# A four-layer graph network on one core: the norm's last step tied behind masks, three kinds of transposes later, half of the feature sums later

## The chip, the cores and the metric

The kernel runs on one core of one Trainium2 chip. The time is the device time of one execution in microseconds (us); a comparison uses the median of several executions. The kernel before has a median of 2874.45 us over three runs (2873.52 to 2877.68).

Five engines work in parallel, each through its own queue in a fixed order: TensorE (PE, matmuls; PEld is its weight load), VectorE (DVE), ScalarE (ACT), GpSimd (POOL) and SyncE (SP, which here only issues transfers). An instruction that has to wait for another engine or for a transfer also holds everything behind it in its own queue. In what follows, times such as "at 2463.23" are microseconds from the start of the profiled execution, and L354 is line 354 of the kernel before.

## The reference

There are 2708 nodes with 512 features each, and a dense 2708 x 2708 matrix `adj`, mostly zeros. Four layers follow each other, each of the form `x = layernorm(x + layer(x))`. Cut to what matters:

```
deg = max(sum(adj != 0, axis=1), 1)
# layer 0: weighted sum over neighbours; each non-zero gets 1/sqrt(count) added
head = mask(adj > 0) / sqrt(row count);  inc = adj + head
y0 = (inc @ x) / rowsum(inc)
# layer 1: attention over the non-zeros, a second convolution, two gates
h = x @ W_sa;  s_left = h @ a[:512];  s_right = h @ a[512:]
e = where(adj != 0, exp(-leaky_relu(s_left[:,None] + s_right[None,:])), 0)
y1 = sigmoid(gate_a * (e @ h / (rowsum(e) + 1e-5)) + gate_b * (adj @ (x @ W_gcn) + b_gcn))
# layer 2: three hops
p = x;  out = x @ w[0];  for i in 1..3: p = adj @ p; out += p @ w[i]
# layer 3: normalised convolution with self loops
y3 = relu((D^-1/2 (adj + I) D^-1/2 @ x + x) @ W + b)
```

Everything is in 32-bit floats. The products of `adj` (or of something of its shape) with a 2708 x 512 matrix are by far the largest part.

## The kernel before, in words

**Products.** The nodes are split in two halves of 1354, the features in two halves of 256. So `adj` is a 2 x 2 array of blocks (called 11, 12, 21, 22 in the code), and the features are four blocks B11, B12, B21, B22. A product of two such arrays is done in the manner of Strassen and Winograd, with seven block products in place of eight. For that, sums of blocks are needed on both sides: of the features (T1 to T4, made on VectorE), and of the adjacency (called z, s or a, made from loaded tiles on VectorE, L403 and L1226). T1 = B12 - B11, T2 = B22 - T1, T3 = B22 - B12 (it takes the place of B12), T4 = B21 - T2. In the tiles, a name such as T3A is the part A of the rows of T3.

**Stages.** A stage is a sweep over ranges of columns of the result; `S[s]` is 28 s on an axis of positions. Layer 0 is the sweep at S[0] (about 0 to 430 us), layer 1 has two sweeps at S[1] and S[2] (430 to 1300 us), the hops and layer 3 are sweeps of a second kind (`sweep2`, at S[3] to S[6]), which splits the rows once more with a second level of seven products; the last, S[6], is from about 2490 us to the end. Its range of 338 columns is processed as group g, product j, with `u` the length of one step.

**Order.** Each piece of work is an event, put down with `at(pos, fn, hold)`. Events are sorted by position and emitted in that order. For the first part of the list (positions below START = 5, and what follows up to three times as many instructions) each engine's queue is in the order of the list. Behind it, the scheduler sets the order, with the list as priority; an event with `hold=True` is tied behind the instruction before it in the list on the same engine. The order is fixed when the kernel is built, and every execution replays it.

**The pieces that the change touches:**

- `next_x2(base, ...)` loads the next sweep's features, and `sums(g)` (L346 to L357) makes T1, T2, T3, T4 of one part g = A, C, B, D in one event, by four subtractions L352 to L355 on VectorE, held at position base + 4.2 + 0.3 i.
- `sweep(...)`, with `plain` for the first range of layer 0: `pw` is the position of the preparing instructions of its blocks "21" and "22" (L779 and L780: a weight row times a tile, and its sum with the tile, on VectorE).
- `layernorm(dsts, y, w, on_scalar)` (L553 to L567): statistics on VectorE (L555, L557, L559), a power on POOL (L560), a product on VectorE (L562), and the last step either on ScalarE (L565) or on VectorE (L567). `done0` calls it for each finished tile of layer 0, after adding the product (L838), and stores the tile in X1.
- Counting in layer 0: masks of the non-zeros are made on ScalarE (L712, L713) or VectorE (L710); TensorE sums them (cnt, L724); the result becomes a row of roots, r (L753), which `spread_row` transposes on TensorE (pr, L761) and copies on ScalarE (row, L764) for L779 of the next range.
- In layer 1, `score_rows` and `rows` (in `extra1`) both call `to_rows`: a transpose on TensorE (ps_r, L937) of the scores s_left (L929) or of the reciprocal degrees rdeg (L999), a copy on ScalarE (L939) and a store from POOL (L940).
- In `sweep2`, L1217 loads z, `add_diag` (L1240) adds the diagonal to it, L1226 makes the sums z and s, L1260 those of the features (t), L1281 are the matmuls into the accumulators accu, accc, accd, acca, and L1299 and L1305 take these out into q. L1317 adds two q. The rest of the rows goes through accr (L1352, L1356) and is added in L1363. ps_n (L1388) is a transpose of a finished q for the norm; L635, L645 and L654 are the dense products of the last layer (d or q, ps, z).

Of the kernel before, what the change touches and what calls it, by code (L numbers as in the profile page):

```python
# [24 lines left out]
ALU = mybir.AluOpType  # L25
# [43 lines left out]
def gnn_kernel(ctx: ExitStack, tc: tile.TileContext, x, adjT, w_sa, a_sa, w_gcn, b_gcn, wab, bab, w_hop, w_out,  # L69
# [232 lines left out]
    def next_x2(base, src, ext_src=None, one=False, plus=False, swapped=False):  # L302

        q = nc.gpsimd
        m = RANGES2[1][0] // P
        early = {"B11": (-5.8, m), "B12": (-4.8, m)}
        late = 2.3 if base == S[6] else 1.6
        if one:
            early["B22"] = (-0.95, RANGES[-1][0] // P)

        def go(s, ks, ext):
            for k in ks:
                x_load(src, k, s, q)
            if ext and ext_src is not None:
                c0 = HD if s in ("B12", "B22") else 0
                for i, g in enumerate("BD"):
                    r0 = (HD if s in ("B21", "B22") else 0) + i * P
                    h = "T3" if s == "B12" else s
                    if g == "D" and ks[-1] < 8:
                        group(h, g)  # L320
                    t, w = groups[h, g][0][:, 2, :], ext_src[r0 : r0 + P, :]
                    if not swapped:
                        nc.scalar.dma_start(out=t, in_=w[:, c0 : c0 + HD])
                        continue
                    for f in range(2):
                        nc.scalar.dma_start(out=t[:, f * P : (f + 1) * P].rearrange("p (c d) -> p c d", d=32),
                                            in_=w.rearrange("p (c f d) -> p f c d", c=4, d=32)[:, c0 // P + f, :, :])

        def residual(s):

            for i, g in enumerate("BD"):
                t = groups[s, g][0][:, 2, i * P : (i + 1) * P]
                nc.vector.tensor_tensor(t, t, ident, ALU.add)

        if plus:
            at(base - 1.4, lambda: residual("B22"), True)
            at(base + 1.9, lambda: residual("B11"), True)
        for s, p in (("B22", 0.0 if one else -1.95), ("B21", 0.02), ("B11", late), ("B12", late + 0.15)):
            ks = list(range(KW))
            if s in early:  # L340
                lo, m = early[s]
                at(base + lo, lambda s=s, m=m: go(s, range(m), True))
                ks = range(m, KW)
            at(base + p, lambda s=s, ks=ks: go(s, ks, ks[0] == 0))

        def sums(g):  # L346
            i = slice(0, 2 if g in "BD" and ext_src is None else 3)
            part = lambda t: t[:, i, :]
            for s in ("T1", "T2", "T4"):
                group(s, g)  # L350
            t = {s: part(groups[s, g][0]) for s in SETS}
            nc.vector.tensor_tensor(t["T1"], t["T3"], t["B11"], ALU.subtract)  # L352
            nc.vector.tensor_tensor(t["T2"], t["B22"], t["T1"], ALU.subtract)
            nc.vector.tensor_tensor(t["T3"], t["B22"], t["T3"], ALU.subtract)  # L354
            nc.vector.tensor_tensor(t["T4"], t["B21"], t["T2"], ALU.subtract)  # L355
            for s in ("T1", "T2", "T3", "T4"):
                groups[s, g][1].update(range(3))  # L357

        def rest():
            for e in range(2):  # L360
                cols = slice(e * HD, (e + 1) * HD)
                for s in REST_HOMES[e]:
                    group(s, "R")
                t, t32 = (groups[s, "R"][0] for s in REST_HOMES[e])
                lo, hi = src[KT - 1], src[2 * KT - 1]
                rows_over(q, t, (lo[:, cols], hi[:, cols]))
                q.dma_start(out=t32, in_=copies(hi[KA - KR :, cols], 4))

        at(base + late + 0.15, rest)
        for i, g in enumerate("ACBD"):  # L370
            at(base + 4.2 + 0.3 * i, lambda g=g: sums(g), True)


    def sweep(base, ranges, prep=None, extra=None, done=None, first=False, late=None, sums=False, save=False):
        A, spare = {}, {}
        nk = KW
        for r, (R0, n) in enumerate(ranges):
# [34 lines left out]
            pw = {ij: (p + 0.3, f) for ij, (p, f) in when.items()}  # L412
            if plain:
                when = {"11": (-4.0, 0.2), "12": (-3.8, 0.2), "21": (-2.4, 0.4), "22": (-1.6, 0.4)}
                pw = {"11": (-0.9, 0.6), "12": (-0.3, 0.6), "21": (3.3, 0.9), "22": (4.1, 0.9)}
            for ij in ("11", "21", "22", "12"):
                for k in ks:
                    p, f = when[ij]
# [131 lines left out]
                     [(h * KT + k, k * P - R0, wt(k)) for k in ts])  # L550


    def layernorm(dsts, y, w, on_scalar=False):  # L553
        st = small.tile([P, 6], F32, name="st")
        nc.vector.bn_stats(st[:w], y[:w])  # L555
        mv = small.tile([P, 2], F32, name="mv")
# [5 lines left out]
            nc.vector.scalar_tensor_tensor(rstd[:w, 0:1], mv[:w, 0:1], -1.0, rstd[:w, 1:2], ALU.mult, ALU.mult)  # L562
        for d, c0, c1 in dsts:
            if on_scalar:
                nc.scalar.activation(d[:w], y[:w, c0:c1], AF.Identity, bias=rstd[:w, 0:1], scale=rstd[:w, 1:2])  # L565
                continue
            nc.vector.tensor_scalar(d[:w], y[:w, c0:c1], mv[:w, 0:1], rstd[:w, 1:2], ALU.subtract, ALU.mult)  # L567

# [226 lines left out]
    def extra0(pb, r, R0, n, A):  # L795
        if r == 0:
            for h, p, d in ((0, -3.7, 0.05), (1, 1.9, 0.055)):
# [9 lines left out]
                    at(pb + (1.7 if h == 0 else 4.8) + 0.06 * j,  # L807
                       lambda h=h, i=i, a=a: add_run(R0, h, n, count_rows(R0, i), a()))
                at(pb + p + d * 22, lambda h=h: count_row(R0, n, h))
                at(pb + p + d * 22 + 0.1 * h, lambda h=h: spread_row(R0, n, h))  # L810
        if r + 1 < len(RANGES0):
            R1, n1 = RANGES0[r + 1]
            for h, p, d in ((0, 1.0, 2.5), (1, 3.8, 2.5)) if r else ((0, 3.2, 2.2), (1, 5.4, 2.1)):
                for i in range(NT):
                    q = pb + p + d * i / NT
                    at(q - 0.7, lambda i=i, h=h: count_load(R1, n1, h, i))
                    at(q - 0.35, lambda i=i, h=h: count_mask(R1, n1, h, i))
                    count_three(q, R1, n1, h, range(NT), i)
                at(pb + p + d, lambda h=h: count_row(R1, n1, h))
                at(pb + p + d + 0.15, lambda h=h: spread_row(R1, n1, h))  # L820

        def inverse(o, s, t, w):
            nc.vector.reciprocal(o, s)
# [4 lines left out]
    def done0(p0, dp, last, R0, n, h, C, tiles):  # L828
        for i, (t, lo, w) in enumerate(tiles):
# [5 lines left out]
            def b(t=t, lo=lo, w=w, got=got):  # L835
                ps = untranspose(C, h, lo, w)
                y = got["x"]
                nc.vector.scalar_tensor_tensor(y[:w], ps[:w], rd[t][:w], y[:w], ALU.mult, ALU.add)  # L838
                o = targets(t, last and not h, "o")
                layernorm(o, y, w, not last)  # L840
                store(X1[t], o, w)

            p = p0 + dp * i + (0.0 if last and not h else 0.2)
            at(p - 0.3, a)
            at(p, b)

    def start0():
        ws = load_w(w_sa)
# [105 lines left out]
    i = 0  # L954
    for R0, n in RANGES:
        for h in (1, 0):
# [5 lines left out]
                at(S[1] + 1.1 + 0.95 * i, lambda t=h * KT + k, w=wt(k): score(t, w, got1))  # L962
                i += 1
            at(S[1] + 1.12 + 0.95 * (i - 1), lambda R0=R0, h=h, ts=tiles_of(R0, n): scores_end(R0, h, ts))
            at(S[1] + 1.6 + 0.95 * (i - 1), lambda R0=R0, h=h, ts=tiles_of(R0, n): score_rows(R0, h, ts))
    at(S[1] + 1.13 + 0.95 * (i - 1), scores_over)

    def extra1(pb, r, R0, n, A):
# [34 lines left out]
                    DROW[h][0, ts[0] * P : (ts[-1] + 1) * P].rearrange("(k i) -> k i", i=P))  # L1003

        at(pb + 2.6, lambda: end(1))
        at(pb + 3.2, lambda: rows(1))
        at(pb + 5.2, lambda: end(0))
        at(pb + 5.8, lambda: rows(0))

    def done1(p0, dp, last, R0, n, h, C, tiles):  # L1010
        Z = {}
# [183 lines left out]
    def sweep2(base, ext, done, on_diag=False):  # L1195
        nk = K2 + ext
        u = 2 / 7
        for g, (i0, n) in enumerate(RANGES2):
            Q, C = {}, {}
            for j, m in enumerate(ORDER2[g]):  # L1200
# [41 lines left out]

                for p, q, pos in ((0, 0, -0.52), (1, 0, -0.51), (1, 1, 0.59), (0, 1, 4.04)):
                    for k in range(nk) if on_diag and op != "12" else ():
                        at(b + u * (pos + 0.8 * k / nk), lambda p=p, q=q, k=k, f=add_diag: f(p, q, k))

                def tsum(nm, x, y, T=T, st=st, nk=nk):

# [366 lines left out]
```

## Time and profile before

| | us |
|---|---|
| median of 3 runs (lowest, highest) | 2874.45 (2873.52, 2877.68) |
| the profiled execution's own time | 2874.17 |
| its span, first to last instruction | 2872.1 |
| mean granted TensorE clock | 0.998 |
| TensorE busy | 2826.4 (98%) |
| VectorE busy | 2197.7 (77%) |
| ScalarE busy | 546.3 (19%) |
| POOL busy | 617.6 (22%) |
| longest single wait of TensorE | 4.4 |

Read the busy times first: they say which engine there is almost no room on. The list of waits then says for how long TensorE stood still, for which line of which engine, how often and how long at the longest. A line of a timeline gives the start, the duration, the engine, the line of the kernel, the operation, what it writes and reads, the shapes and how many like it follow each other; in brackets at its end is the idle time of the engine just before it and what ended that.

### The profile page before, as it was taken

Reading aid. Unit: us, or ns where it says so; the run is one execution under the profiler, and the core shown is the slowest. Engines: PE = TensorE matmul, PEld = TensorE weight load, DVE = VectorE, ACT = ScalarE, POOL = GpSimd, SP = SyncE. Lnnn points to the kernel's source line nnn. Section 1 sums busy time; section 2 is a strip of 40 time slices with the busy share of each in tenths; the row PEclk is TensorE's granted clock in tenths of the full one; section 3 lists DMA queues with packets and bytes.
Section 4 is the critical chain, followed back from the end, with each engine's and each line's share of the span. In section 5 each row is a group of like instructions: output and inputs, shape, how many; then the busy total and the mean of one; then the engine's idle time right before and its main releaser. Section 6 shows DMA issues by size and latency. Waiting matters only on the chain. (4 is left out here: it accounts for less than half of the span.)

```text
span 2872.1 us, 37476 instructions
## 1 busy us (share of the span) xinstructions
PE 2826.4 (98%) x10963; PEld 1870.2 (65%) x10963; DVE 2197.7 (77%) x5670; ACT 546.3 (19%) x1119; POOL 617.6 (22%) x1113
## 2 busy tenths in 40 slices
PE   7999999999999999999999999999999999999998
PEld 5656665658765656766666666666666666666665
DVE  6989799667636554655699788887888878799987
ACT  4554200101146444641100000000000100100001
POOL 0223233223310101123213033030330211501202
PEclk9999999999999999999999999999999999999999
DMA  7666466355534333565668667566675665754542
GB/s 232 204 200 191 143 213 225 114 163 167 191 107 135 111 115 97 168 193 153 202 203 242 204 193 239 172 209 197 198 234 173 187 196 177 228 172 146 177 141 92
DMA packets 368524, 510.04 MB, mean 178 GB/s; under 512 B 63424, under 2 KB 321700, under 8 KB 368320
## 3 DMA queue, kind: packets, MB, share of 16 engines
q1 hardware_dynamic: 302392, 370.56, 43.8%
q0 software_dynamic: 49344, 126.38, 13.1%
q10 hardware_dynamic: 16584, 10.71, 1.3%
q8 instruction: 87, 1.43, 0.2%
q14 instruction: 117, 0.96, 0.1%
HBM read 423.77 MB, written 83.65 MB: 177 GB/s over the span
## 5 line engine op out<-in xcount | busy, mean ns | idle before, releaser
L1226 DVE TENSOR_TENSOR z<-z 128x339 f32<-128x339 f32 (+1 forms) x966 | 454.6, 504 | 12.6 <-PE accu L1281 3.4
L1299 ACT COPY q<-accu 128x338 f32<-128x338 f32 (+1 forms) x84 | 34.6, 443 | 1004.5 <-PE accu L1281 1002.7
L560 POOL TENSOR_TENSOR rstd<-rstd,neg_half 128x1 f32<-128x1 f32 (+3 forms) x91 | 59.3, 652 | 755.8 <-DVE rstd L559 494.9
L1281 PE MATMUL accc<-s,t 128*128 128x338 f32 (+1 forms) x644 | 198.2, 450 | 0.0
L1281 PE MATMUL accu<-z,t 128*128 128x338 f32 (+1 forms) x644 | 194.0, 448 | 1.5 <-DVE z L1226 1.5
L1281 PE MATMUL accd<-z,t 128*128 128x338 f32 (+1 forms) x644 | 193.9, 448 | 0.6 <-DVE q L1363 0.6
L1281 PE MATMUL accc<-z,t 128*128 128x338 f32 (+1 forms) x644 | 193.5, 448 | 0.5 <-ACT q L1299 0.5
L1414 POOL DMA_DIRECT2D Y<-y x192 | 105.0, 553 | 366.7 <-DVE y L1409 333.7
L403 DVE TENSOR_TENSOR a<-a,a 128x384 f32<-128x384 f32 (+2 forms) x330 | 162.6, 511 | 22.5 <-PE accu L458 21.7
L1281 PEld LDWEIGHTS accc<-s,t 128*128 128x128 f32 x644 | 120.9, 190 | 64.1 <-issue 7.5
L1281 PEld LDWEIGHTS accc<-z,t 128*128 128x128 f32 x644 | 122.0, 190 | 61.6 <-issue 1.0
L1281 PEld LDWEIGHTS accu<-z,t 128*128 128x128 f32 x644 | 121.7, 190 | 61.7 <-DVE z L1226 2.0
L1281 PEld LDWEIGHTS accd<-z,t 128*128 128x128 f32 x644 | 121.9, 190 | 60.5 <-DVE q L1363 1.5
L1226 DVE TENSOR_TENSOR s<-z 128x338 f32<-128x338 f32 (+1 forms) x322 | 149.7, 503 | 12.7 <-PE accc L1281 8.4
L1305 DVE TENSOR_TENSOR q<-q,accd 128x338 f32<-128x338 f32 (+1 forms) x112 | 56.0, 500 | 115.1 <-PE accd L1281 115.1
L1082 DVE SCALAR_TENSOR_TENSOR a<-a,e 128x384 f32<-128x384 f32 (+2 forms) x160 | 77.4, 507 | 51.0 <-ACT e L1081 46.3
L1080 ACT ACTIVATE e<-row,s_right 128x384 f32<-128x384 f32 (+5 forms) x176 | 96.5, 569 | 76.1 <-PE accc L458 20.4
L979 DVE SCALAR_TENSOR_TENSOR deg<-a,deg 128x384 f32<-128x384 f32 (+2 forms) x152 | 75.8, 505 | 13.6 <-DMA a<-in_adjT 11.9
L406 POOL DMA_DIRECT2D As<-a x120 | 64.9, 544 | 73.0 <-DVE a L403 70.2
L779 DVE SCALAR_TENSOR_TENSOR s<-a,row 128x384 f32<-128x384 f32 (+2 forms) x152 | 75.1, 507 | 6.0 <-ACT row L764 6.0
L1081 ACT ACTIVATE e<-e 128x384 f32<-128x384 f32 (+5 forms) x176 | 79.4, 477 | 1.8
L606 PE MATMUL ps_d<-w,xT 128*128 128x512 f32 (+1 forms) x176 | 79.2, 593 | 0.4 <-ACT xT L597 0.4
(683 smaller groups left out, 5840.4 us busy)
## 6 DMA issues: line engine op xcount, KB each, us to landing
z<-As SPq DMA_DIRECT2D x320, 169.5 KB
z<-As SPq DMA_DIRECT2D x320, 169.0 KB
a<-in_adjT SPq DMA_DIRECT2D x240, 192.0 KB
z<-in_adjT SPq DMA_DIRECT2D x240, 169.5 KB
z<-in_adjT SPq DMA_DIRECT2D x240, 169.0 KB
a<-in_adjT SPq DMA_DIRECT2D x120, 165.0 KB
a<-in_adjT SPq DMA_DIRECT2D x112, 128.0 KB
As<-a POOLq DMA_DIRECT2D x60, 192.0 KB, 3.9
```

Of the source, the lines that this page charges most:

```text
L403: nc.vector.tensor_tensor(A[r, dst, k][:, :n], A[r, a, k][:, :n], A[r, b, k][:, :n], op)
L406: nc.gpsimd.dma_start(out=SD[m][k * P : (k + 1) * P, R0 : R0 + n], in_=A[r, dst, k][:, :n])
L560: nc.gpsimd.tensor_tensor(rstd[:w, 1:2], rstd[:w, 0:1], neg_half[:w], ALU.pow)
L606: nc.tensor.matmul(o, lhs(c), r, start=c == 0 and n == 0, stop=c == DC - 1, skip_group_check=True)
L779: nc.vector.scalar_tensor_tensor(t[:w, :n], a[:w, :n], 0.0, row[R0, h][:w, :n], ALU.is_gt, ALU.mult)
L979: nc.vector.scalar_tensor_tensor(d[:w, :n], a[:w, :n], 0.0, d[:w, :n], ALU.not_equal, ALU.add)
L1080: nc.scalar.activation(e[:w, :n], row[R0, h][:w, :n], AF.Prelu, bias=s_right[:w, t : t + 1], alpha=0.01)
L1081: nc.scalar.activation(e[:w, :n], e[:w, :n], AF.Exp, scale=-1.0)
L1082: nc.vector.scalar_tensor_tensor(a[:w, :n], a[:w, :n], 0.0, e[:w, :n], ALU.not_equal, ALU.mult)
L1226: nc.vector.tensor_tensor(d[:, :n], Z[x + (k,)][:, :n], Z[y + (k,)][:, :n], op)
L1281: nc.tensor.matmul(B[home][:, :n], stat(v, k), a[:, :n], start=bool(start and k == 0), stop=k == nk - 1, skip_group_check=True)
L1414: nc.gpsimd.dma_start(out=rows[:, :, f * P : (f + 1) * P], in_=o[32 * f : 32 * (f + 1), : m * P].rearrange("p (b d) -> p b d", d=P))
```

## The change

Six edits, all of them to positions and ties. No operation is added or removed.

1. `sums(g)` is split in three events: T1 and T2 stay at base + 4.2, T3 moves to base + 7.4, T4 to base + 9.2 (each + 0.3 i for the parts A, C, B, D), all held.
2. The preparing instructions of the blocks "21" and "22" of the first range are 0.1 later.
3. The last step of layer 0's norm (L565), where it is on ScalarE, becomes an event of its own at p + 0.28, held behind what stands before it on ScalarE; the store into X1 is put at the same position.
4. `spread_row` is later: by 0.08 for one of the two halves of the first range, by 0.1 and 0.25 for those of the next ranges.
5. In layer 1, `score_rows` goes from +1.6 to +2.3, and `rows` from +3.2 and +5.8 to +3.7 and +6.3.
6. In `sweep2`, `add_diag` of the very first product (g = j = 0) is held. Only S[6] has the diagonal on.

```diff
-        def sums(g):
+        def sums(g, n):
             i = slice(0, 2 if g in "BD" and ext_src is None else 3)
             part = lambda t: t[:, i, :]
-            for s in ("T1", "T2", "T4"):
-                group(s, g)
+            if n == 0:
+                for s in ("T1", "T2", "T4"):
+                    group(s, g)
             t = {s: part(groups[s, g][0]) for s in SETS}
-            nc.vector.tensor_tensor(t["T1"], t["T3"], t["B11"], ALU.subtract)
-            nc.vector.tensor_tensor(t["T2"], t["B22"], t["T1"], ALU.subtract)
-            nc.vector.tensor_tensor(t["T3"], t["B22"], t["T3"], ALU.subtract)
-            nc.vector.tensor_tensor(t["T4"], t["B21"], t["T2"], ALU.subtract)
-            for s in ("T1", "T2", "T3", "T4"):
-                groups[s, g][1].update(range(3))
+            if n == 0:
+                nc.vector.tensor_tensor(t["T1"], t["T3"], t["B11"], ALU.subtract)
+                nc.vector.tensor_tensor(t["T2"], t["B22"], t["T1"], ALU.subtract)
+                for s in ("T1", "T2", "T3", "T4"):
+                    groups[s, g][1].update(range(3))
+            elif n == 1:
+                nc.vector.tensor_tensor(t["T3"], t["B22"], t["T3"], ALU.subtract)
+            else:
+                nc.vector.tensor_tensor(t["T4"], t["B21"], t["T2"], ALU.subtract)
...
         for i, g in enumerate("ACBD"):
-            at(base + 4.2 + 0.3 * i, lambda g=g: sums(g), True)
+            for n, p in enumerate((4.2, 7.4, 9.2)):
+                at(base + p + 0.3 * i, lambda g=g, n=n: sums(g, n), True)
...
-                pw = {"11": (-0.9, 0.6), "12": (-0.3, 0.6), "21": (3.3, 0.9), "22": (4.1, 0.9)}
+                pw = {"11": (-0.9, 0.6), "12": (-0.3, 0.6), "21": (3.4, 0.9), "22": (4.2, 0.9)}
...
-    def layernorm(dsts, y, w, on_scalar=False):
+    def layernorm(dsts, y, w, on_scalar=False, late=None):
...
             if on_scalar:
-                nc.scalar.activation(d[:w], y[:w, c0:c1], AF.Identity, bias=rstd[:w, 0:1], scale=rstd[:w, 1:2])
+                fn = lambda d=d, c0=c0, c1=c1: nc.scalar.activation(d[:w], y[:w, c0:c1], AF.Identity,
+                                                                    bias=rstd[:w, 0:1], scale=rstd[:w, 1:2])
+                fn() if late is None else late.append(fn)
                 continue
...
-                at(pb + p + d * 22 + 0.1 * h, lambda h=h: spread_row(R0, n, h))
+                at(pb + p + d * 22 + 0.18 * h, lambda h=h: spread_row(R0, n, h))
...
-                at(pb + p + d + 0.15, lambda h=h: spread_row(R1, n1, h))
+                at(pb + p + d + (0.25 if h else 0.4), lambda h=h: spread_row(R1, n1, h))
...
-                o = targets(t, last and not h, "o")
-                layernorm(o, y, w, not last)
-                store(X1[t], o, w)
+                got["o"] = o = targets(t, last and not h, "o")
+                layernorm(o, y, w, not last, None if last else got.setdefault("late", []))
+                if last:
+                    store(X1[t], o, w)
+
+            def c(t=t, w=w, got=got):
+                for fn in got["late"]:
+                    fn()
...
+            if not last:
+                at(p + 0.28, c, True)
+                at(p + 0.28, lambda t=t, w=w, got=got: store(X1[t], got["o"], w))
...
-            at(S[1] + 1.6 + 0.95 * (i - 1), lambda R0=R0, h=h, ts=tiles_of(R0, n): score_rows(R0, h, ts))
+            at(S[1] + 2.3 + 0.95 * (i - 1), lambda R0=R0, h=h, ts=tiles_of(R0, n): score_rows(R0, h, ts))
...
-        at(pb + 3.2, lambda: rows(1))
+        at(pb + 3.7, lambda: rows(1))
...
-        at(pb + 5.8, lambda: rows(0))
+        at(pb + 6.3, lambda: rows(0))
...
-                        at(b + u * (pos + 0.8 * k / nk), lambda p=p, q=q, k=k, f=add_diag: f(p, q, k))
+                        at(b + u * (pos + 0.8 * k / nk), lambda p=p, q=q, k=k, f=add_diag: f(p, q, k), g == j == 0)
```

## The prediction

> **What bounds the kernel now.** I read the table of busy time first, then the list of what TensorE waited for, then the timelines of the places named there, and the granted clock by window.
>
> ```profile
> PE 2826.4 (98%) x10963; PEld 1870.2 (65%) x10963; DVE 2197.7 (77%) x5670; ACT 546.3 (19%) x1119; POOL 617.6 (22%) x1113
> ```
>
> TensorE is busy for 2826.4 of 2872.1 us, so an edit that only reorders work has 45.7 us to win at the very most. 7.4 us of these lie behind the last matmul. The changed kernel, built, has the same instructions, matched one to one, in another order within each engine's queue; what I say below of an order after the change is that built order. So everything hangs on the single waits:
>
> ```profile
> PE pr L761 <- DVE r L753: 5.7, 4, 2.0
> PE cnt L724 <- ACT mask L713: 3.6, 2, 2.6
> PE accd L1281 <- DVE z L1226: 2.5, 6, 1.0
> PE ps_n L1388 <- DVE q L1305: 1.8, 1, 1.8
> ...
> PE ps_r L937 <- DVE s_left L929: 1.6, 1, 1.6
> PE ps_r L937 <- DVE y L652: 1.6, 1, 1.6
> PE accu L1281 <- DVE z L1226: 1.5, 1, 1.5
> ...
> PE accd L1281 <- DVE q L1363: 0.6, 1, 0.6
> ```
>
> Columns: total us, times, longest. Each line is something that the diff moves or that stands beside it: 18.9 us in all. Why they arise shows on the other engines, with the idle time and its releaser in brackets (ScalarE, then VectorE):
>
> ```profile
> 75.47 0.81 ACT L565 ACTIVATE o<-ld,rstd 128x512 f32<-128x512 f32 x1 [2.90 <-DVE rstd L562]
> ...
> 81.31 0.81 ACT L565 ACTIVATE o<-ld,rstd 128x512 f32<-128x512 f32 x1 [2.12 <-DVE rstd L562]
> ```
>
> ```profile
> 2463.23 0.27 DVE L1240 SCALAR_TENSOR_TENSOR z<-ident,diag,z 128x46 f32<-128x46 f32 x1 [5.12 <-DMA z<-As]
> ...
> 2518.54 0.95 DVE L354 TENSOR_TENSOR T3A<-B22A,T3A 128x768 f32<-128x768 f32 x1
> 2519.41 0.95 DVE L355 TENSOR_TENSOR T4A<-B21A,T2A 128x768 f32<-128x768 f32 x1
> ...
> 2574.75 0.51 DVE L1305 TENSOR_TENSOR q<-q,accd 128x338 f32<-128x338 f32 x1 [2.63 <-PE accd L1281]
> ...
> 2580.36 0.51 DVE L1305 TENSOR_TENSOR q<-q,accc 128x338 f32<-128x338 f32 x1 [0.41 <-PE accc L1281]
> ...
> 2583.20 0.51 DVE L1305 TENSOR_TENSOR q<-q,accd 128x338 f32<-128x338 f32 x1 [0.44 <-PE accd L1281]
> ...
> 2605.41 0.48 DVE L654 SCALAR_TENSOR_TENSOR z<-ps,rdeg_f,z 128x256 f32<-128x256 f32 x1 [2.10 <-PE ps L645]
> ```
>
> In the first, ScalarE stands still for a norm while the masks that TensorE wants are queued behind it. In the second, VectorE stands still for 5.12 us for a load that only a diagonal needs. Gaps of TensorE also cost clock; the columns are busy us of PE, PEld, DVE, ACT, POOL, then the granted clock:
>
> ```profile
> 80.00:84.00 4.00, 1.47 (x7) 0.95 (x5) 3.13 (x12) 2.63 (x6) 1.17 (x2) 1.00 0.42 99
> 84.00:88.00 4.00, 3.89 (x21) 3.06 (x22) 3.79 (x11) 3.87 (x10) 0.00 (x0) 0.59 0.92 298
> 88.00:92.00 4.00, 2.05 (x18) 1.57 (x17) 3.45 (x14) 2.90 (x8) 0.00 (x0) 0.93 1.03 351
> 92.00:96.00 4.00, 4.00 (x16) 3.15 (x16) 3.79 (x11) 3.87 (x10) 0.00 (x0) 0.63 0.21 63
> ```
>
> The gap of 2.64 us that ends at 84.11 and the one of 1.95 us that ends at 90.96 are each followed by about 3.4 us at half clock. Eight 128x256 matmuls took 3.64 us there, four took 1.03 us right after, so each window costs 3.64 - 2 x 1.03, about 1.6 us. The gaps of 1.84, 1.59 and 1.58 us later were followed by none. [...]
>
> **The change, part by part.** All sums are against the profiled execution, 2874.17 us (span 2872.1 and 2.07 around it), which is 0.28 below the median of the runs.
>
> *Layer 0: norm's last step behind masks, and root transposes later.* With L565 behind further masks, ScalarE no longer loses 2.90 and 2.12 us ahead of them. The mask that TensorE got at 84.05 is there at about 79.1; TensorE comes for it at 81.47. The gap of 2.64 goes, and its slow window of 1.6: 4.2 us. But the row transpose (pr, 90.96) is bound by VectorE, which is dense from 72.7 to 164 and does not get faster: one pair L779/L780 (two slots of 0.4) now stands behind the L838 that waits for TensorE until 72.72, so r is ready at about 91.7 and not 90.90. The transpose moved behind nine counts and six matmuls, 2.6 us of work, and so TensorE is about 2 us ahead once it is done; in place of 1.95 there is a gap of about 2.9, and its slow window stays. So 2.0 us are left of it. Two things take them back. VectorE's lead over TensorE at 154.5 was 2.88, so no more than about 2 can be kept; and the load of va (issued by ScalarE, L854) now stands behind eight more mask operations, lands 1.7 us later (VectorE already waited 0.36 us for it at 163.97), and the first L403 behind it is ready at about 166.8 where TensorE comes at 165.0: 1.8 us. In the later ranges, the row transposes go behind one or two matmuls of 0.5 to 0.65 us; VectorE, which waited 3.41 us for such a row at 329.00, is 1.3 us later, less 0.8 that it no longer waits for POOL's power: the gap of 1.22 + 0.27 + 0.27 at 365 grows by 0.4. SP's fetches stand up to 18 us earlier, ahead of loads of a, whose leads are 15 us or more. Sum: -2.0 + 1.8 + 0.4 = +0.2. Ends: -4.2, if the transpose's chain keeps up; +4, if the new gap of 2.9 and the stall of 1.8 (near the 1.95 that did it) each bring another slow window of 1.6.
>
> *Layer 1: transposes of scores and degrees later (L937).* They move behind 5 to 16 us of matmuls (477.44 to about 485, 581.77 to about 591). s_left and the freed bank are there long before: 1.59 + 1.58 = 3.2 us. Behind the moved copies (L939) on ScalarE stand gates and U copies whose own releasers are as late, one excepted (661.63, 0.3 us late, feeding a store); the stores of rows on POOL (L940) feed reads much later. What can take it back is the gap of 0.79 at 725.45 (pg), since VectorE waits for TensorE no more between 669.5 and 729; but its waits there (1.99 for ld) are for loads that are released by the same engines, so they move along. I take -3.2; ends 0 and -3.2.
>
> *Hops: T3 and T4 of the feature sums later.* At 1443.72, 1806.36 and 2167.62, TensorE waits 0.26 each for a z behind T3D and T4D. With these behind it the gaps go: -0.8. They run 40 to 60 us later, where VectorE waits for TensorE (2.1 us in four pieces around 1490 to 1500) and its leads are 4 to 8 us; the stationaries are first used behind that. Ends 0 and -0.8.
>
> *Last layer, start.* The tied diagonals stand behind q<-accd, so VectorE no longer loses 5.12 us; the z at 2463.97 (0.22) and 2468.44 (0.96) and the q for ps_n (1.84) come in time: -3.0. It does wait for accd first (about 3 us), so its lead ahead of the next gaps is about 2 us, not 5. T3A, T4A, T3C, T4C (four slots of 0.87) and the B and D pieces (four of 0.60) no longer stand ahead of the z for 2528.86 (1.48) and 2535.35 (0.54): -2.0. Together -5.0; ends -5.0 and -2.0 (the second alone).
>
> *Last layer, the price.* The T4 pieces now run behind 2574.75, the point at which VectorE has caught up with TensorE (it waited 2.63). Behind it come 2 x 0.87 + 2 x 0.60 = 2.9 us of T4 and 0.8 of diagonals that had run before; only 0.41 + 0.44 of waits and a few waits of 0.1 to 0.2 between absorb them. Adding slot by slot, VectorE reaches the first d (2588.64) 2.2 us later against TensorE, and is dense from there to the q that accd waits for at 2601.38 (0.59). One matmul of 0.43 is moved ahead of that wait: 2.2 - 0.43 = +1.7. The wait of 2.10 at 2605.41 then resets VectorE. Ends 0 and +3.0.
>
> Sum: +0.2 - 3.2 - 0.8 - 5.0 + 1.7 = -7.1; 2874.17 - 7.1 + 0.28 gives 2867.3 us, 0.25% faster.
>
> **Rivals.** About 0.2% (5.7 us) is what a measurement of this kernel tells from no change.
>
> 1. Given back. VectorE is the second bound (77%): the gap at 725 takes the 3.2 of layer 1, or the one at 2601 grows to its end. For it: VectorE's dense stretches; against: leads above 4 us elsewhere. 2867.3 + 3.2 = 2870.5, no change.
> 2. Slower: SP's queue. X1's stores follow the late norm, and a fetch that was moved ahead waits for such a store (206.49 and about 312) and holds the loads of a behind it for some 4.4 us. Where their lead is under 4.4 us, TensorE stalls 4.4, with a slow window of 1.6: two places in layer 0 are 12 us, 2879.3; a third makes 2885. Against it: leads of 15 us.
> 3. Layer 0 keeps its 4.2 and the next gap of 1.95 goes with its window: 2867.3 - 0.2 - 4.2 - 3.5 = 2859.4. Against it: r is bound by VectorE.
> 4. The gap of 2.9 in the row's wait brings no slow window: 1.6 less, 2865.7. [...]
>
> **How the numbers follow.** The forecast has 0.47 (its own range 2864.5 to 2870.0), rival 1 0.27, rival 2 0.12, rival 3 0.08, rival 4 0.06. Faster by over 0.2% (under 2868.7): 0.42 of the forecast, rivals 3 and 4, 0.56. Within: the rest of it and rival 1, 0.32. Slower: 0.12. The range leaves out rivals 2 and 3 and reaches from 2862.9 (layer 0 keeping its 4.2) to 2875.6 (rival 1, with layer 0 at +4 and the price at 2601 at +3.0).
>
> **What would show it.** After: no wait of cnt for ACT near 84 and one slow window, not two; a wait of pr of 2 to 3 us near 90; no waits of ps_r; no VectorE wait of 5 us for z<-As near 2463, and none of ps_n; accd's wait for q L1363 grown from 0.6 to about 2. The forecast is wrong if the wait of pr or of L403 in layer 0 is much longer, if pg's wait near 725 grows to 3 to 4, or if a load of a ends waits of TensorE.

## The result, and the profile after

The changed kernel takes 2866.06 us (median of 8 runs, 2864.66 to 2869.84) against 2874.89 us before (8 runs beside them, 2873.52 to 2877.87). The ratio is 0.9969, with a 95% interval of 0.9959 to 0.9980. The forecast was 2867.3, faster by 0.25%. The profiled execution took 2867.6 us with a span of 2865.5. So the total came out, but not all of its parts: layer 0 came out 3.2 to 3.8 us worse than forecast, layer 1 and the start of the last layer together about 3 us better. That these misses nearly cancel is luck, and runs of one kernel scatter by 4 us or more besides.

Line numbers of the changed kernel are larger: L713 is L720 there, L753 is L760, L403 is L408, L1363 is L1378, L565 is L570. In the other kernels below the numbers differ again by a few lines; the names of the tiles are the same. The table of busy time after:

```profile
PE 2826.0 (99%) x10963; PEld 1871.7 (65%) x10963; DVE 2196.1 (77%) x5670; ACT 544.3 (19%) x1119; POOL 616.7 (22%) x1113
```

TensorE's work is the same; only its waits are other ones. The list of what TensorE waited for (total, times, longest; the waits of cnt for VectorE's masks, 11.2 us in all against 11.6 before, are left out):

```profile
...
PE pr L768 <- DVE r L760: 4.3, 3, 2.6
PE accd L463 <- DVE a L408: 4.1, 5, 1.9
PE cnt L731 <- ACT mask L720: 3.9, 5, 1.4
PE ps L652 <- DVE z L661: 1.9, 4, 0.8
PE accd L1296 <- DVE q L1378: 1.8, 1, 1.8
...
```

The waits of ps_r, ps_n and of accu and accd for z, 9.0 us before, are gone from it. The longest wait of pr grew from 2.0 to 2.6, accd's for a from 1.2 to 1.9, and accd's for q from 0.6 to 1.8. ScalarE's norms and what the gap did to the clock show in its timeline and in the windows (busy us of PE, PEld, DVE, ACT, POOL, then the granted clock):

```profile
74.95 0.81 ACT L570 ACTIVATE o<-ld,rstd 128x512 f32<-128x512 f32 x1 [0.95 <-DVE rstd L567]
...
80.78 0.82 ACT L570 ACTIVATE o<-ld,rstd 128x512 f32<-128x512 f32 x1 [2.11 <-DVE rstd L567]
```

```profile
84.00:88.00 4.00, 3.16 (x23) 2.48 (x22) 3.80 (x10) 2.37 (x5) 0.00 (x0) 1.00 1.02 359
88.00:92.00 4.00, 1.37 (x6) 0.62 (x4) 3.42 (x15) 1.77 (x5) 0.00 (x0) 0.92 0.26 83
92.00:96.00 4.00, 3.69 (x18) 2.77 (x17) 3.79 (x10) 3.90 (x9) 0.00 (x0) 0.50 0.67 190
96.00:100.00 4.00, 4.00 (x11) 2.59 (x11) 0.93 (x4) 3.37 (x9) 0.25 (x1) 0.50 0.43 129
```

The first norm now waits 0.95 in place of 2.90; the second still waits 2.11, but with the needed mask ahead of it. The gap of 2.64 near 84 is gone (the longest wait for a mask there is 0.84, ending at 85.52), and the clock stays at 1.00. But behind the next gap the clock is at half from 91.3 to 101.6. TensorE's waits in the timeline:

```profile
91.22 0.83 PE L768 MATMUL pr<-ident,r 128*128 128x128 f32 x3 [2.63 <-DVE r L760]
...
156.73 1.56 PE L463 MATMUL accd<-a,T1C 128*128 128x384 f32 x4 [1.33 <-DVE a L408]
...
368.90 1.38 PE L463 MATMUL accd<-a,T1C 128*128 128x330 f32 x4 [1.92 <-DVE a L408]
...
2594.96 1.41 PE L1296 MATMUL accd<-z,t 128*128 128x338 f32 x4 [1.78 <-DVE q L1378]
```

And on VectorE, at the start of the last layer:

```profile
2465.35 0.51 DVE L1320 TENSOR_TENSOR q<-q,accd 128x339 f32<-128x339 f32 x1 [2.91 <-PE accd L1296]
2465.77 0.34 DVE L1255 SCALAR_TENSOR_TENSOR z<-ident,diag,z 128x128 f32<-128x128 f32 x1
2466.15 0.51 DVE L1241 TENSOR_TENSOR s<-z 128x338 f32<-128x338 f32 x1
```

The diagonals follow q<-accd now. The wait of 5.12 us for the load of z is gone; in its place VectorE waits for TensorE (2.91), which is harmless, since TensorE is then the one that works.

**Where the time went.** To see this per stage, I take the same matmul in two profiles and subtract its starts. The table gives by how much this shift changes from one position (on the time axis of the kernel before) to the next, as the median over the matmuls of the 6 us that begin there. The last column is a second profile of the changed kernel, taken later.

| stretch, us | forecast | after | after, again |
|---|---|---|---|
| 0 to 60 (queues as before) | 0 | -0.5 | +1.5 |
| 60 to 430, layer 0 | +0.2 | +4.0 | +3.4 |
| 430 to 1440, layer 1 | -3.2 | -4.4 | -4.7 |
| 1440 to 2440, hops | -0.8 | -1.0 | -0.2 |
| 2440 to 2545, last layer's start | -5.0 | -6.8 | -6.8 |
| 2545 to 2605, the price | +1.7 | +1.8 | +1.8 |
| 2605 to the end | 0 | +0.3 | +0.3 |

### The profile page after: what moved, and what is told of

Its sections match the earlier page's. It is cut to its first block, busy times and chain, and to the rows that moved or that the text cites. A ratio compares the mean times of both kernels' runs of the same rounds, so it can differ in the third digit from the quotient of the medians.

```text
span 2865.5 us, 37473 instructions
## 1 busy us (share of the span) xinstructions
PE 2826.0 (99%) x10963; PEld 1871.7 (65%) x10963; DVE 2196.1 (77%) x5670; ACT 544.3 (19%) x1119; POOL 616.7 (22%) x1113
## 4 chain that ended last, share of the span: by engine, by line
PE 87%; DVE 7%; issue 2%; DMA 2%; SPq 1%; POOL 1%; ACT 1%; DVEq 0%; POOLq 0%; ACTq 0%
PE accu L1296 12%; PE accd L1296 12%; PE accc L1296 12%; PE accd L463 8%; PE accu L463 8%; PE accc L463 8%; PE ps_d L613 6%; PE acca L1296 6%; PE acca L463 4%; PE accr L1367 2%; PE ps L652 2%; PE accr L1371 1%; DVE z L1241 1%; DVE z L661 1%; DVE s L786 1%
## 5 line engine op out<-in xcount | busy, mean ns | idle before, releaser
L1241 DVE TENSOR_TENSOR z<-z 128x339 f32<-128x339 f32 (+1 forms) x966 | 454.2, 501 | 11.2 <-PE accu L1296 3.1
L565 POOL TENSOR_TENSOR rstd<-rstd,neg_half 128x1 f32<-128x1 f32 (+3 forms) x91 | 59.8, 658 | 754.9 <-DVE rstd L564 507.4
L408 DVE TENSOR_TENSOR a<-a,a 128x384 f32<-128x384 f32 (+2 forms) x330 | 161.9, 508 | 23.3 <-PE accu L463 22.6
```

Of the source, the lines that this page charges most:

```text
L408: nc.vector.tensor_tensor(A[r, dst, k][:, :n], A[r, a, k][:, :n], A[r, b, k][:, :n], op)
L1241: nc.vector.tensor_tensor(d[:, :n], Z[x + (k,)][:, :n], Z[y + (k,)][:, :n], op)
```

## The experiments

Two things have to be known first. The times scatter: the kernel before gave 2870.93 to 2882.21 in 26 runs on one chip. And much of that can arise early: among profiles of kernels that have the same queues up to 60 us, TensorE was between 1.1 us ahead and 5.1 us behind the kernel before at 60 us. So for parts worth 1 to 5 us I go by the shift from 60 us on, and use the times as a check of the sum. In kernels with layer 0 unchanged, the shift from 60 to 430 us was -0.5 to +1.1 (six profiles); that is the resolution. For a part of it, 60 to 110 us, it is coarser: -1.7 to +1.0 in the same six. In the four kernels with layer 1 unchanged, the shift over layer 1 was -0.9 to +1.8.

The theory was the forecast's: each wait that a moved instruction explains goes, at the price of a few named ones, and layer 0 is no gain. The rival was that layer 0 is a gain, as the removed wait of 2.64 us suggests, and that what looks like a loss is chance. The first four kernels were run together.

### Layer 0's edits alone: l0_only

The kernel before with edits 2, 3 and 4 of the change, without 1, 5 and 6:

```diff
-                pw = {"11": (-0.9, 0.6), "12": (-0.3, 0.6), "21": (3.3, 0.9), "22": (4.1, 0.9)}
+                pw = {"11": (-0.9, 0.6), "12": (-0.3, 0.6), "21": (3.4, 0.9), "22": (4.2, 0.9)}
...
-                o = targets(t, last and not h, "o")
-                layernorm(o, y, w, not last)
-                store(X1[t], o, w)
+                got["o"] = o = targets(t, last and not h, "o")
+                layernorm(o, y, w, not last, None if last else got.setdefault("late", []))
+                if last:
+                    store(X1[t], o, w)
...
+            if not last:
+                at(p + 0.28, c, True)
+                at(p + 0.28, lambda t=t, w=w, got=got: store(X1[t], got["o"], w))
...
-                at(pb + p + d * 22 + 0.1 * h, lambda h=h: spread_row(R0, n, h))
+                at(pb + p + d * 22 + 0.18 * h, lambda h=h: spread_row(R0, n, h))
...
-                at(pb + p + d + 0.15, lambda h=h: spread_row(R1, n1, h))
+                at(pb + p + d + (0.25 if h else 0.4), lambda h=h: spread_row(R1, n1, h))
```

> The kernel before with the layer 0 edits alone (norm's last step tied, root transposes later, blocks 21 and 22 prepared 0.1 later). Theory A, from the shift of TensorE's work between the two traces: the wait of cnt near 84 goes, but the wait of pr near 91 grows to about 2.6 us and is followed by two slow windows, and VectorE is later at 157 and 365; layer 0 ends about 4 us later, so 2879 us (2876 to 2881), slower than before. Theory B: layer 0 is a gain as the removed wait of 2.64 us suggests, and what is seen of a loss is the phase of the clock's windows: 2870 to 2873 us.

2878.70 us against 2876.41, ratio 1.0008 (0.9999 to 1.0017). From 60 to 430 us TensorE lost 2.6 us. The wait of pr was 2.64 and was followed by two half-clock windows (94.8 to 101.6); the longest wait for `a` was 1.9. So the three edits together are no gain and, by the trace, a loss; the interval of the times alone does not exclude none.

### The change without layer 0's edits: no_l0

The kernel before with edits 1, 5 and 6 of the change; of 5 and 1 the core is shown:

```diff
-            at(base + 4.2 + 0.3 * i, lambda g=g: sums(g), True)
+            for n, p in enumerate((4.2, 7.4, 9.2)):
+                at(base + p + 0.3 * i, lambda g=g, n=n: sums(g, n), True)
...
-        at(pb + 3.2, lambda: rows(1))
+        at(pb + 3.7, lambda: rows(1))
...
-                        at(b + u * (pos + 0.8 * k / nk), lambda p=p, q=q, k=k, f=add_diag: f(p, q, k))
+                        at(b + u * (pos + 0.8 * k / nk), lambda p=p, q=q, k=k, f=add_diag: f(p, q, k), g == j == 0)
```

> The changed kernel without its layer 0 edits: sums split, layer 1's transposes later, last layer's first diagonal tied. Theory A: layer 1 -4.4, hops -1.0 to -1.6, last layer -6.8 + 1.8, so about 2874.9 - 10.7 = 2864 us (2862.5 to 2866), 2 to 4 us below the changed kernel. Theory B (layer 0 is a gain): 2868 us or more, above the changed kernel's 2866.1.

2868.34 us, ratio 0.9965 (0.9953 to 0.9978): above the forecast range, with its runs from 2864.02 to 2869.22, and by the times no better than the changed kernel: the median lies where the rival had put it (2868 us or more). By the trace, the span is 2861.9, with -0.1 from 60 to 430 us and -9.0 behind it. Taken as ratios, 0.9965 here and 0.9969 for the changed kernel, the times cannot tell the two theories apart; the trace speaks for the first.

### Layer 1's transposes alone: tr_only

```diff
-            at(S[1] + 1.6 + 0.95 * (i - 1), ... score_rows(R0, h, ts))
+            at(S[1] + 2.3 + 0.95 * (i - 1), ... score_rows(R0, h, ts))
-        at(pb + 3.2, lambda: rows(1))
+        at(pb + 3.7, lambda: rows(1))
-        at(pb + 5.8, lambda: rows(0))
+        at(pb + 6.3, lambda: rows(0))
```

> The kernel before with layer 1's transposes later, alone. Theory A: the two waits of ps_r go and TensorE is 3.2 us (by the idle time) to 3.6 us (by the shift) ahead, and about as much is left at the end: 2871.3 us (2870.5 to 2872). Rival: VectorE is dense from 670 to 729, and the wait of pg near 725 takes it back: 2874 to 2875 us.

2870.51 us, ratio 0.9979 (0.9969 to 0.9988). Both waits of ps_r are gone. The shift has a step of -1.9 at each of them (477 and 582), though the idle times were 1.59 and 1.58, and is -4.6 over layer 1. Nothing is taken back at 725, so the rival falls. The wait of pg there is gone as well, but that is not the edit's doing: it is gone too in l0_only, norm_only and spread_only, where layer 1 is that of the kernel before, and these gain 0.8 to 1.6 us from 700 to 735. What the two removed waits give is the two steps, 3.7 us.

### The tied diagonal alone: diag_only

```diff
-  at(b + u * (pos + 0.8 * k / nk), lambda p=p, q=q, k=k, f=add_diag: f(p, q, k))
+  at(b + u * (pos + 0.8 * k / nk), lambda p=p, q=q, k=k, f=add_diag: f(p, q, k), g == j == 0)
```

> The kernel before with the last layer's first diagonal tied, alone. Theory A: VectorE's wait of 5.12 us for z<-As goes, and TensorE's waits near 2464, 2468 and 2477 with it; TensorE is 4.1 us ahead by 2490, more than the 3.0 us of idle time. The sums still stand ahead of the z at 2529 and 2535, where VectorE's lead is about 2 us, so the waits there stay or grow by up to 2: 2871 to 2873 us. Rival: VectorE's work sets those waits alone, and they grow by all that was won: 2874 to 2875 us.

2871.25 us, ratio 0.9978 (0.9969 to 0.9986). From 2440 to 2485 us the shift is -4.1, as expected. But the waits at 2529 and 2535 did not stay: they are gone too, and the shift is -6.0 by 2545. So this one tie brings most of what the last layer's start wins, and the split of the sums is not needed there. I had put these 2.0 us down to the sums.

### The norm's tie alone: norm_only

The next four were run together.

The kernel before with edit 3 alone:

```diff
-                o = targets(t, last and not h, "o")
-                layernorm(o, y, w, not last)
-                store(X1[t], o, w)
+                got["o"] = o = targets(t, last and not h, "o")
+                layernorm(o, y, w, not last, None if last else got.setdefault("late", []))
+                if last:
+                    store(X1[t], o, w)
...
+            if not last:
+                at(p + 0.28, c, True)
+                at(p + 0.28, lambda t=t, w=w, got=got: store(X1[t], got["o"], w))
```

> The kernel before with the norm's last step tied behind masks, alone; the root's transpose stays where it was. Theory A (the transpose waits for VectorE's r at about 91.5, whatever ScalarE does): the wait of cnt near 84 goes, and TensorE stands at pr for about 5 us instead, followed by two or three slow windows (of 3.4 us, 1.7 lost each); between 60 and 110 us TensorE loses 1 to 4 us against the kernel before. Theory B (ScalarE's masks were the bound): pr waits 2 us or less, and TensorE gains 4 us there.

2874.72 us, ratio 1.000 (0.9991 to 1.001). TensorE's timeline, then the clock:

```profile
91.83 0.90 PE L763 MATMUL pr<-ident,r 128*128 128x128 f32 x3 [5.75 <-DVE r L755]
```

```profile
84.00:88.00 4.00, 2.06 (x11) 1.51 (x11) 3.83 (x11) 3.70 (x8) 0.00 (x0) 1.00 0.86 263
88.00:92.00 4.00, 0.17 (x1) 0.18 (x2) 3.45 (x14) 1.20 (x4) 0.00 (x0) 0.59 0.75 278
92.00:96.00 4.00, 4.00 (x21) 3.35 (x22) 3.73 (x10) 3.87 (x9) 0.00 (x0) 0.55 0.56 148
96.00:100.00 4.00, 4.00 (x28) 2.96 (x27) 4.00 (x13) 3.53 (x10) 0.44 (x1) 1.00 0.04 6
```

The wait near 84 is gone and is waited for again at pr, 5.75 us in one piece, because r comes from VectorE at 91.8 whatever ScalarE does. From 60 to 110 us nothing is won or lost (0.0, where unchanged kernels spread from -1.7 to +1.0); the loss of 1 to 4 that was expected does not show. Part of the two half-clock windows (88.7 to 95.6) lies in the gap itself, where a slow clock costs nothing.

### The root transposes alone: spread_only

The kernel before with edit 4 alone:

```diff
-                at(pb + p + d * 22 + 0.1 * h, lambda h=h: spread_row(R0, n, h))
+                at(pb + p + d * 22 + 0.18 * h, lambda h=h: spread_row(R0, n, h))
...
-                at(pb + p + d + 0.15, lambda h=h: spread_row(R1, n1, h))
+                at(pb + p + d + (0.25 if h else 0.4), lambda h=h: spread_row(R1, n1, h))
```

> The kernel before with the root transposes later, alone; the norm as before. Theory A: the wait of cnt near 84 (2.6 us) and its slow window stay; the wait of pr near 91 (1.95) is covered by the 2.6 us of work that now stands ahead, and goes with its slow window: TensorE gains 3 to 3.7 us between 60 and 110 us, and loses about 1 near 365. Theory B (the two edits only work together): pr waits 1.5 us or more all the same, with a slow window, and nothing is gained.

2873.46 us, ratio 0.9995 (0.9986 to 1.0004). TensorE's timeline, then the clock:

```profile
84.70 0.38 PE L724 MATMUL cnt<-ones_bf,mask 128*128 128x1 bf16 x9 [2.63 <-ACT mask L713]
...
91.55 0.54 PE L761 MATMUL pr<-ident,r 128*128 128x128 f32 x3
```

```profile
84.00:88.00 4.00, 3.24 (x24) 2.49 (x24) 3.79 (x11) 3.84 (x10) 0.00 (x0) 1.00 0.77 239
88.00:92.00 4.00, 3.43 (x24) 2.72 (x24) 3.45 (x14) 2.92 (x7) 0.00 (x0) 1.00 0.87 280
92.00:96.00 4.00, 3.40 (x24) 2.45 (x24) 3.76 (x10) 3.87 (x10) 0.00 (x0) 1.00 0.71 194
```

The wait near 84 stays, as in the kernel before, but pr does not wait at all: the work that now stands ahead of it covers the 1.95 us. From 60 to 110 us it is -3.8, to 430 us -2.8. The interval of the times holds no change and this gain both; the same edit is in the best kernel below, where it shows again. One thing was not expected: the gap of 2.63 us is followed by no half-clock window here (the clock is 1.00 from 84 to 96), where the gap of 2.64 before was followed by one of 3.41 us. What makes the difference was not shown. The gain does not rest on it: the best kernel below has a window behind this gap (85.9 to 89.3) and the same -3.8, while here TensorE waits 0.63 and 0.60 for masks at 88.57 and 92.69 that it does not wait for there.

So the two edits of layer 0 are not two gains. Alone, the later transpose is worth 3 to 4 us between 60 and 110. With the norm's tie as well, TensorE comes to pr earlier than r can be there, and stands in one long gap behind which the clock is low.

### T4 early in the last layer: t4_early

On the kernel no_l0:

```diff
-            for n, p in enumerate((4.2, 7.4, 9.2)):
+            for n, p in enumerate((4.2, 7.4, 7.8 if base == S[6] else 9.2)):
```

> The changed kernel without its layer 0 edits, and with T4 of the last layer's features at base + 7.8 in place of 9.2: all of T4 then stands ahead of q<-accd, where VectorE had waited 2.6 us. Theory A (the T4 behind that point made accd's wait for q L1363): that wait falls from 1.8 us to 0.6 or less, and TensorE is 1.2 to 1.8 us ahead of the version without layer 0 edits from there on, with no new wait of TensorE at 2550 to 2590. Rival (the diagonals behind that point made it): the wait falls by 0.8 us at the most.

2865.03 us, ratio 0.9964 (0.9951 to 0.9976). TensorE's timeline:

```profile
2589.91 1.13 PE L650 MATMUL ps<-w,q 128*128 128x256 f32 x4 [0.48 <-DVE z L659]
...
2592.39 1.40 PE L1286 MATMUL accd<-z,t 128*128 128x338 f32 x4 [1.35 <-DVE q L1368]
```

The wait for q falls by 0.4 from no_l0's 1.78, less than theory A wanted, and the wait for z ahead of it grows from 0.33 to 0.48: +1.8 from 2545 to 2605, no better than with T4 late. So T4 behind the point where VectorE has caught up is not the only way to pay. VectorE waits 0.23 and 1.24 us there now, ahead of q<-accd and q<-acca, with the five sums s and the t of T3 queued behind these; in the kernel before, the first two t stood ahead of both and four of the s between them, where they filled the wait.

### The sums split in the hops alone: sums_hops

On the kernel no_l0:

```diff
-            for n, p in enumerate((4.2, 7.4, 9.2)):
+            for n, p in enumerate((4.2, 4.2, 4.2) if base == S[6] else (4.2, 7.4, 9.2)):
```

> The changed kernel without its layer 0 edits, and with the sums of the last layer as before; they are split in the hops alone. The diagonal is tied. Theory A, from the tied diagonal alone: TensorE's waits at 2464 to 2477 go (4.1 us), of those at 2529 and 2535 about 0.8 us is left or comes back, and accd waits 0.6 us for q L1363, not 1.8: 0.5 to 1.5 us ahead of the version with all sums split. Rival (the sums' split is what the last layer needs): 2 us or more behind it.

2863.51 us (four runs), ratio 0.9962 (0.9947 to 0.9977). TensorE's timeline:

```profile
2591.56 1.40 PE L1286 MATMUL accd<-z,t 128*128 128x338 f32 x4 [0.60 <-DVE q L1368]
```

The price is gone: +0.1 from 2545 to 2605, and -6.0 from 2440 to 2545 where the split sums gave -6.8. On balance, the split in the last layer costs 0.9 us by the trace.

### T3 where it was, T4 late: t3_now

Run with the two below.

On the kernel no_l0:

```diff
-            for n, p in enumerate((4.2, 7.4, 9.2)):
+            for n, p in enumerate((4.2, 4.2 if base == S[6] else 7.4, 9.2)):
```

> The changed kernel without its layer 0 edits, and with T3 of the last layer's features back at base + 4.2, T4 at 9.2. Theory A (work that the sums push behind 2574, of T4 above all, makes accd's wait for q L1363): the wait stays near 1.8 us, since T4 is where it was. Rival (T3 in VectorE's dense stretch at 2560 to 2570 makes it, by delaying what came behind): the wait falls to 0.6.

2866.96 us, ratio 0.9969 (0.9959 to 0.9979).

```profile
2596.39 1.40 PE L1286 MATMUL accd<-z,t 128*128 128x338 f32 x4 [2.14 <-DVE q L1368]
```

With T4 alone late, the wait is 2.14, about as much as no_l0's 0.33 for z and 1.78 for q together; by the shift the price is +1.5. So late T4 is enough for the price, as the forecast had it; early T4 with late T3 does not take it away. Both observations stand, and the price is that of an order in which VectorE's spare time ahead of 2574 isn't used, not of four instructions. Which other piece would have to move for t4_early to be free of it was not tried.

### The changed kernel again: after_again

The kernel of the result, unedited, for a second profile of its layer 0.

> The changed kernel once more, on the same chip as the two above. Theory A (layer 0's edits are a loss): between 60 and 430 us TensorE ends 2.5 to 4 us later than in the kernel before, as in the first profile, whatever the phase of the clock's windows; the number of slow windows behind the wait of pr (three in the first profile) may differ. Theory B (the loss was the phase): 0 to 1 us.

2868.73 us, ratio 0.9975 (0.9966 to 0.9984). From 60 to 430 us +3.4. The clock:

```profile
88.00:92.00 4.00, 2.63 (x12) 1.97 (x11) 3.76 (x12) 0.47 (x1) 0.00 (x0) 1.00 0.73 255
92.00:96.00 4.00, 2.41 (x15) 1.83 (x16) 3.42 (x14) 3.67 (x9) 0.00 (x0) 0.67 0.39 102
96.00:100.00 4.00, 4.00 (x11) 2.35 (x10) 2.48 (x7) 3.33 (x9) 0.00 (x0) 0.50 0.53 134
100.00:104.00 4.00, 4.00 (x19) 3.05 (x19) 2.11 (x6) 2.90 (x8) 0.54 (x1) 0.55 0.46 141
```

Three windows again, from 93.4 to 103.6. That layer 0's edits lose is not the chance of one profile: with l0_only it is three, +4.0, +3.4 and +2.6, against -0.5 to +1.1 in the kernels without them.

### What the parts suggest together: best

The kernel before with edits 4, 5 and 6 of the change, and with edit 1 in the hops only (on the kernel no_l0):

```diff
-                at(pb + p + d * 22 + 0.1 * h, lambda h=h: spread_row(R0, n, h))
+                at(pb + p + d * 22 + 0.18 * h, lambda h=h: spread_row(R0, n, h))
...
-                at(pb + p + d + 0.15, lambda h=h: spread_row(R1, n1, h))
+                at(pb + p + d + (0.25 if h else 0.4), lambda h=h: spread_row(R1, n1, h))
...
-            for n, p in enumerate((4.2, 7.4, 9.2)):
+            for n, p in enumerate((4.2, 4.2, 4.2) if base == S[6] else (4.2, 7.4, 9.2)):
```

> The kernel before with the root transposes later (layer 0), layer 1's transposes later, the sums split in the hops alone and the last layer's first diagonal tied; the norm's last step and the last layer's sums as before. Theory, adding the shifts of TensorE measured for each part: layer 0 -2.8, layer 1 about -4, hops -1.6, last layer -6, so 2874.9 - 14 = 2861 us (2859 to 2864), below both kernels. Rival (the parts don't add, since what is won in layer 0 is waited for again in layer 1): 2863.5 us or more, as the same kernel without the later root transposes.

2860.69 us (2859.04 to 2863.61), against 2875.96 before and 2868.73 for the changed kernel beside it. The ratio to before is 0.9950 (0.9937 to 0.9962). It beats both. Against sums_hops (0.9962), which lacks only edit 4, the intervals of the ratios overlap; that edit 4 adds to it rests on the trace. The shift goes by the parts: +0.2 up to 60 us, -2.9 in layer 0, -3.9 in layer 1, -2.5 in the hops, -6.0 at the last layer's start and +0.1 for the price, -15.0 in all by the end, which is the difference of the spans (2857.1 against 2872.1). The -2.5 of the hops is more than the change has there (-1.0); the three steps of the split are -1.6 of it in both, and the rest is the spread between profiles. What TensorE waits for:

```profile
...
PE cnt L729 <- ACT mask L718: 4.7, 3, 2.6
PE pr L766 <- DVE r L758: 3.1, 2, 1.7
PE accd L463 <- DVE a L408: 2.6, 5, 1.0
...
PE accd L1286 <- DVE q L1368: 0.6, 1, 0.6
...
```

## Why the prediction was right

The total was right (2867.3 against 2866.06), and most of the mechanisms were, with one term of the sum missized by 3 to 4 us and two others by 1 to 2 the other way. That the total is this close is the luck of these misses.

- **Layer 0, the chain.** The forecast said that the wait near 84 goes, that pr is bound by VectorE and waits about 2.9, that the first L403 behind the load of va stalls TensorE by 1.8, and that the waits at 365 grow by 0.4. Measured: pr waits 2.63. VectorE does wait longer for va (1.26 in place of 0.36), but TensorE's wait behind that load is only 0.22, at 169.68. A stall of 1.33 stands earlier, at 156.73, ahead of the load: the L408 that ends it comes at 156.14 in a stretch where VectorE works without a break, and the lead of 2.88 that VectorE had at that matmul in the kernel before is used up. The size was about right (+1.6 by the shift between 120 and 215), the place and the cause were not. The waits at 365 grew by 1.0 in idle time (1.2 by the shift). That r bounds pr is shown by norm_only and spread_only, which take the two edits apart.
- **Layer 0, the clock: the step that failed.** It said "its slow window stays", one window of 1.6 behind the gap of 2.9. There were three in both profiles of the changed kernel, some 10.2 us at half clock, which is 5.1 lost where the kernel before lost 3.4 in all. The forecast's range had layer 0 at +4 as its upper end; the sum took +0.2. The difference, 1.6 expected to go and 1.7 added in its place, is 3.3 of the 3.8 us by which layer 0 is worse than forecast. The shift agrees: from 60 to 110 us it is +1.2, where the forecast's terms up to there give -2.0. Why three windows came and not one stays open.
- **Layer 1.** Right in kind. -3.2 was too small: the steps are -1.9 each, and pg's wait went instead of growing. That fear, rival 1, has not come; but pg's wait goes in kernels with layer 1 unchanged too, so what lies beyond 3.7 of the measured 4.4 and 4.7 is not the edit's.
- **Hops.** The three waits of 0.26 went. Each step of the shift is -0.53, in every kernel that has the split there. Over the whole stretch the seven profiles with the split in the hops give -0.2 to -2.5, up to 1.4 us off from the -1.6 of the three steps, nearly all of it between 1500 and 1600 us and from causes not looked into; kernels without the split show -0.3 to +1.0 over the stretch.
- **Last layer's start.** All five waits went, -6.8 in place of -5.0. But by diag_only and sums_hops the tie of the diagonal does 6.0 of it, and the sums 0.8. The attribution of the last 2.0 us to T3 and T4 was wrong; without the stand of 5.12 us, VectorE was early enough for them.
- **The price.** +1.7 forecast, +1.8 measured, in the place named. With the sums of the last layer as before it is +0.1, so the split causes it. That T4 is what does it holds when T4 alone is late, but putting T4 early did not remove it.
- **The rivals.** SP's fetches ahead of the loads of `a` (rival 2) did nothing: no load of `a` ends a wait of TensorE. Rival 3, all of the 4.2 us kept and the next gap gone, fell with the trace of the changed kernel (pr waits 2.63, layer 0 is +4.0), and norm_only shows why. Rival 4 took a gap of 2.9 to bring no low clock; it fell, since both profiles of the changed kernel show half clock behind the wait of pr (2.63 us in the first), from 91.3 to 101.6 and from 93.4 to 103.6.

**Why the idle times were too small.** The sums of idle times gave 3.2 for layer 1 and 3.0 for 2464 to 2477; the shifts are 3.7 and 4.1. The difference is in how the trace counts. Back to back, matmuls of 339 columns start 0.285 us apart, and the trace lets each last 0.45. From the start at 2463.03 to the one at 2469.11 there are fourteen steps, 6.08 us in the kernel before, where 14 x 0.285 is 3.99. So 2.09 were lost (the shift there is -2.1), but the listed idle times are 0.22 and 0.96. Where a matmul waits while the one ahead of it still lasts in the trace, no idle time is shown at all.

## What to carry to other kernels

Before a wait is removed, ask which engine bounds the next one in line: in norm_only the masks were freed, TensorE came 5.75 us early to a row that another engine had not made, and two stops became one longer stop. A stop can cost more than its length, by the slow clock behind it (10.24 us at half clock behind the gap of 2.63 us in the changed kernel), so two edits that each look like a gain need to be measured singly; the one that moves the waiting instruction behind other work was the one to keep. And an instruction that waits for a transfer in the middle of a busy in-order queue is worth a tie of its own: one such tie won 6.0 us by the trace, where the whole change won 8.8 by the times.

## What was not expected of the hardware

- Whether half clock follows a gap of TensorE is not told by the length of the gap alone. Behind a gap of 2.63 us there was no window (spread_only), behind 2.64 one (the kernel before, 84.73 to 88.14, 3.41 us, 1.7 of them lost), behind 2.64 two (l0_only, 94.8 to 101.6) and behind 2.63 three (the changed kernel, 91.33 to 101.57, 10.24 us). A gap of 1.95 us had one behind it (the kernel before, 91.56 to 94.97); the gap of 1.92 us at 368.90 in the changed kernel and that of 1.84 us at 2476.81 in the kernel before had none. Nor does half clock end as soon as TensorE is busy again. Two stretches of the changed kernel, the first with the gap, in the columns used above:

```profile
87.92:91.33 3.41, 0.78 (x5) 0.36 (x4) 2.90 (x13) 1.13 (x4) 0.00 (x0) 1.00 0.26 93
...
94.75:98.16 3.41, 3.41 (x10) 1.84 (x10) 1.75 (x5) 2.74 (x7) 0.00 (x0) 0.50 0.63 180
```

In the second TensorE is busy throughout, and half clock goes on behind it up to 101.57. What decides whether none, one, two or three windows come, and why it is three in the changed kernel, was not shown.

- The same 60 us of work at the start varied by 6 us between executions, and half-clock windows are a part of it: the clock is at half from 52.0 to 55.4 in t3_now and from 62.3 to at least 68 in t3_now and diag_only, where the kernel before has 1.00 from 20 to 68. How much of the scatter of the times this is, is not shown: the runs without a trace have only a mean clock. Of the five runs of no_l0 the 95% interval of the ratio is 0.0025 wide, 7 us; that is too coarse to tell 2 us apart.
